# Last layer with f32 weights that hold their scales, and four context buffers, in a two-block transformer kernel on one core

## The chip, the core and the metric

The kernel runs on one NeuronCore of a Trainium2 chip. PE is the matrix engine, DVE the vector engine, ACT the scalar engine, POOL is GpSimd, and SP only issues transfers. Each engine executes its instructions in program order and waits on semaphores for what other engines or transfers deliver. Data moves by DMA: SP, ACT and POOL each have a queue, and all queues are served by the same 16 DMA engines. The metric is the time of one execution in microseconds; less is better. The profile's span runs from the first to the last instruction of one profiled execution.

## The reference, cut to what matters

There are 16 batches of 112 rows of 256 numbers, each with a context of 375 rows of 256. Four layers are added to the rows one after the other: attention with 16 heads over the context, a feed-forward layer with two routed experts and a shared one, a second attention with one head over the same context, and a quantized linear layer. Only the last two matter here:

```python
x = x + _L1_xattn_ref(_layernorm(x), ctx_1024, ctx_1024, mask)

# the quantized layer, on x2 = layernorm(x) of all rows
x_scale = jnp.maximum(jnp.abs(x2).max() / 127.0, EPS)
x_int8 = jnp.clip(jnp.round(x2 / x_scale), -128, 127)
acc_i32 = dot(x_int8, weight_int8.T)
out = acc_i32 * x_scale * weight_scale.T + bias
x = x + out
```

The scale of the last layer is one number over all rows of all batches, so no product of that layer can start before the last batch's norm is known.

## The kernel before

All schedules are written out by hand. The first attention is cut into units, four for each batch, and `unit(u)` runs one step. Work of other layers is put beside it with `at(u, f, ...)` and `mid(u, f, ...)`, which hang a call on step `u`. After the last unit the steps go on up to `LAST`: first the slots of the second half of the expert layer, then the second attention of batches 8 to 15.

**The slots.** Rows are sorted by expert into slots of 128 rows. `slot_run` runs one slot, with its expert weights `ew` (two transfers of 1 MB, started by `slot_weights`) and stores its result in `y_s` (`slot_store`). From `FIRST_RUN` on there is one slot in each step, eight in all. Between and after them lie the four quarters of the shared expert for the last chunk of rows (`ph_sh`, `hT_sh`, `acc_sh`). Once all of `y_s` is stored, POOL gathers its rows for each batch (`sort_get`, the tile `got`), and adds them to `x` (`sort_add`, line 843).

**The second attention.** `stages(k)` runs in step `STEP_0 + k`, and works on several batches at once: batch 8+k computes its scores (`second_2`, tiles `pe` and `e`), the one before it transposes its probabilities (`second_3`), the one before that multiplies them with the context (`second_4`) and starts the norm of the last layer (`norm_steps`). A stage later come that norm's rows (`xn_l`) and their largest magnitude (`third_max`). Only then are they transposed into `x3T` (`third_turn`, done four stages after the scores).

Each batch needs its context twice: `ctxT`, transposed, 128 partitions with 3000 bytes each (line 130), and `ctx`, 125 partitions with three pieces of 1024 bytes (line 121). Both are about 384 KB, and SP issues both. There are three buffers for `ctxT` and five for `ctx`. The first three batches' pairs hang on steps `STEP_0 - 7` to `STEP_0 - 5`; from stage 0 on, stage k issues the pair of batch 11+k. The same queue takes the store of the last chunk of `x` (line 804), the loads of batches 13 to 15 from it (`load_xs`, line 809) and, in stage 1, `x3T` for batches 0 to 7, 896 KB (line 1244).

**The last layer.** After the norm of batch 15 the largest magnitude is reduced over partitions by a transpose (`pm`) and spread by a matmul with ones (`pb`), which gives `xscale` and its reciprocal `rscale`. `keep_warm` issues matmuls whose results nobody reads. Then the batches go in eight pairs through three functions: `scaled` multiplies a pair of `x3T` by `rscale` and adds a constant that rounds it (on ACT or DVE); `products` takes the constant off again on ACT, which writes the pair as bf16 (`xi`), and multiplies it with the integer weights `wi_sb` in bf16; `stored` multiplies by `wsx`, the weight scales times `xscale` (DVE), adds the residual (DVE or POOL) and stores the pair.

Of the kernel before, what the change touches and what calls it, by code (L numbers as in the profile page):

```python
# [9 lines left out]
F32 = mybir.dt.float32  # L10
I32 = mybir.dt.int32
BF16 = mybir.dt.bfloat16
I8 = mybir.dt.int8
U8 = mybir.dt.uint8
AF = mybir.ActivationFunctionType
ALU = mybir.AluOpType
# [3 lines left out]
P = 128  # L20
B, S, D = 16, 112, 256
SK = 375
# [4 lines left out]
DC = D // P  # L27
# [10 lines left out]
ROUND = 1.5 * 2.0**23  # L38
# [16 lines left out]
TAIL = 8  # L55
# [3 lines left out]
def tile_kernel(  # L59
# [26 lines left out]
    nc = tc.nc  # L86
# [4 lines left out]
    ctxp = ctx.enter_context(tc.tile_pool(name="ctx", bufs=2))  # L91
# [10 lines left out]
    def gen(name):  # L102
        return ps_gen.tile([P, 512], F32, tag="gen", name=name)
# [3 lines left out]
    xall = const.tile([P, B, D], F32, tag="x", name="x")  # L107
    xt = [xall[:, t, :] for t in range(NT)]
    xs_place = [b if b < B - 4 else b ^ 2 for b in range(B)]
# [7 lines left out]
    ctx_nat, ctxT, ctxT2 = {}, {}, {}  # L117
# [8 lines left out]
        dma.dma_start(out=ctxT[b], in_=ctx_t[b])  # L126

    def load_ctxT2(b):
        ctxT2[b] = late(ctxp, 2, 3, [P, DC, SK], "ctxT_2", f"ctxT2_{b}")
        nc.sync.dma_start(out=ctxT2[b], in_=ctx_t[b])  # L130

    def weight(src, name, dma, pool=wpool):
# [71 lines left out]
    wi_sb = const.tile([P, DC, D], BF16, tag="wi", name="wi")  # L204
# [38 lines left out]
    fin = []  # L243

    def late(pool, bufs, more, shape, tag, name):

        pool, bufs = (fin[0], more) if fin else (pool, bufs)
        return pool.tile(shape, F32, tag=tag, name=name, bufs=bufs)
# [73 lines left out]
    def transposed(dst, src, name):  # L322

        pt = gen(f"pt_{name}")
        n = src.shape[0]
        for c in range(DC):
            nc.tensor.transpose(
                pt[:, c * n : (c + 1) * n], src[:, c * P : (c + 1) * P], ident[:n, :n]
            )
        nc.scalar.copy(dst, pt[:, : DC * n].rearrange("p (c s) -> p c s", c=DC))  # L330
# [571 lines left out]
    x3T = []  # L902
# [10 lines left out]
    def third_turn(bs):  # L913
        for b in bs:
            if b < TAIL:
                t = tmp.tile([P, DC, S], F32, tag="x3s", name=f"x3s_{b}", bufs=1)
                transposed(t, normed["l3", b], f"x3_{b}")
                nc.scalar.dma_start(out=x3T_d[b], in_=t)
            else:
                transposed(x3T[0][:, b, :, :], normed["l3", b], f"x3_{b}")  # L920
# [69 lines left out]
    def small_const(src, name, dtype=F32):  # L990
# [16 lines left out]
        out=wi8_sb, in_=wi8_t.rearrange("(c p) n -> p c n", p=P)  # L1007
# [4 lines left out]
    FIRST_RUN = NU + 6  # L1012
    STEP_0 = FIRST_RUN + NT // 2 + 5
# [4 lines left out]
    def at(u, f, *a):  # L1018
        extra[u].append((f, a))
# [65 lines left out]
    s = sorts[0]  # L1085
# [34 lines left out]
    s = sorts[1]  # L1120
# [41 lines left out]
    for b in range(TAIL, B):  # L1162

        at(FIRST_RUN + 3 if b < 13 else STEP_0 + b - 13, load_xs, b)
    for i in range(3):
        at(STEP_0 - 7 + i, load_ctxT2, TAIL + i)
        at(STEP_0 - 7 + i, load_ctx, TAIL + i)

    make_kT(0, 0, True)
    for i in range(GB):  # L1170
# [56 lines left out]
    def keep_warm(count):  # L1227

        pi = gen("warm")
        for _ in range(count):  # L1230
            nc.tensor.matmul(pi[:, :P], ident, ident, start=True, stop=True)

    for u in range(NU + 3):
# [1 line left out]
    first_att.close()  # L1235
    fin.append(ctx.enter_context(tc.tile_pool(name="final", bufs=1)))
    x3T.append(fin[0].tile([P, B, DC, S], F32, tag="x3T", name="x3T"))
    ws_bc = fin[0].tile([S, D], F32, tag="wscale", name="wscale")
    nc.gpsimd.dma_start(out=ws_bc, in_=wscale.partition_broadcast(S))
    rounding = fin[0].tile([P, 1], F32, tag="rounding", name="rounding")  # L1240
    nc.vector.memset(rounding, ROUND)
    at(
        STEP_0 + 1,
        lambda: nc.sync.dma_start(
            out=x3T[0][:, :TAIL, :, :].rearrange("p b c s -> p b (c s)"),
            in_=x3T_d.rearrange("b p c s -> p b (c s)"),
# [7 lines left out]
    def stages(k):  # L1254
        def b_of(back):
            b = TAIL + k - back
            return b if TAIL <= b < B else None

        def do(back, f):
            b = b_of(back)  # L1260
            if b is not None:
                f(b)

        def norm_steps(name, b):
            nb_on = nc.gpsimd if name == "l2" or b == B - 1 else nc.vector
            steps[name, b] = norm([b], name, True, nb_on)
            for f in steps[name, b][:3]:
                f()

        def now(f, at_k):  # L1270

            for b, own in zip(range(TAIL, B), at_k):
                if own == k:
                    f(b)

        def rows(name):
            return lambda b: steps[name, b][3]()

        no = None
        stats = lambda b: norm_steps("l2", b)  # L1280
        now(sort_get, (-4, -4, -3, -3))
        now(sort_add, (-3, -3, no, no, 1, 2, 3, 4))
        now(stats, (-2,))
        now(rows("l2"), (-1,))
        yield
        now(sort_add, (no, no, -2, -1))
        now(stats, (no, -2))
        if k == -1:
            now(rows("l2"), (no, -1))
            do(-1, second_1)  # L1290
        do(0, lambda b: second_2(b, lambda: do(-1, second_1)))
        do(4, lambda b: third_turn([b]))
        do(1, second_3)
        do(3, rows("l3"))
        now(rows("l2"), (no, no, 0, 1, 2, 3, 4, 5))
        do(2, second_4)
        if k == B - TAIL + 1:

            amax1.append(const.tile([S, 1], F32, tag="amax1", name="amax1"))
            do(3, lambda b: third_max([b]))  # L1300
            nc.vector.tensor_reduce(amax1[0], amax[:, : B - 1], AX.X, ALU.max)
        do(2, lambda b: norm_steps("l3", b))
        now(sort_get, (no, no, no, no, -1, 0, 1, 2))
        now(stats, (no, no, -1, 0, 1, 2, 3, 4))
        if k >= 0:
            do(-3, load_ctxT2)
            do(-3, load_ctx)
        if k != B - TAIL + 1:
            do(3, lambda b: third_max([b]))
        yield  # L1310

    for u in range(NU + 3, LAST - 1):
# [3 lines left out]
        k = u - STEP_0  # L1316
# [12 lines left out]
    d, y = far[0]  # L1329
    amax1 = amax1[0]  # L1330
    nc.vector.scalar_tensor_tensor(amax1, d, y, amax1, ALU.mult, ALU.max)
    pm = gen("pm")
    nc.tensor.transpose(pm[:1, :S], amax1, ident[:S, :S])
    top = const.tile([1, 1], F32, tag="top", name="top")
    nc.vector.tensor_reduce(top, pm[:1, :S], AX.X, ALU.max)
    keep_warm(2)
    pb = gen("pb")
    nc.tensor.matmul(pb[:, :1], ones[0:1, :], top, start=True, stop=True)
    xscale = const.tile([P, 1], F32, tag="xscale", name="xscale")
    nc.vector.tensor_scalar(xscale, pb[:, :1], 1.0 / 127.0, EPS_Q, ALU.mult, ALU.max)  # L1340
    rscale = const.tile([P, 1], F32, tag="rscale", name="rscale")
    nc.vector.reciprocal(rscale, xscale)

    for _ in stages(LAST - 1 - STEP_0):
        pass
    third_turn([B - 1])
    wsx = fin[0].tile([S, D], F32, tag="wsx", name="wsx")
    nc.gpsimd.tensor_scalar(wsx, ws_bc, xscale[:S, :], None, ALU.mult)
    pfs = {}

    def scaled(pair):
        t = x3T[0][:, 2 * pair : 2 * pair + 2, :, :]

        if pair % 2 or pair == 6:
            nc.scalar.activation(t, t, AF.Identity, bias=rounding, scale=rscale)
        else:
            nc.vector.tensor_scalar(t, t, rscale, ROUND, ALU.mult, ALU.add)

    def products(pair):
        t = x3T[0][:, 2 * pair : 2 * pair + 2, :, :]  # L1360
        xi = fin[0].tile([P, 2, DC, S], BF16, tag="xi", name=f"xi_{pair}", bufs=3)
        nc.scalar.add(xi, t, -ROUND)
        pf = gen(f"pf_{pair}")
        for j in range(2):
            for c in range(DC):
                nc.tensor.matmul(
                    pf[:S, j * D : (j + 1) * D],
                    xi[:, j, c, :],
                    wi_sb[:, c, :],
                    start=(c == 0),  # L1370
                    stop=(c == DC - 1),
                )
        pfs[pair] = pf

    def stored(pair):
        y = fin[0].tile([S, 2, D], F32, tag="y", name=f"y_{pair}", bufs=4)
        nc.vector.tensor_tensor(
            y,
            pfs[pair][:S, : 2 * D].rearrange("p (j d) -> p j d", j=2),
            wsx.unsqueeze(1).to_broadcast([S, 2, D]),  # L1380
            ALU.mult,
        )
        first = xs_place[2 * pair]
        add = nc.vector if pair in (2, 5, 7) else nc.gpsimd
        add.tensor_tensor(y, y, xall[:S, first : first + 2, :], ALU.add)
        nc.sync.dma_start(
            out=out[2 * pair : 2 * pair + 2].rearrange("b s d -> s b d"), in_=y
        )

    NP = B // 2  # L1390
    scaled(0)
    scaled(1)
    for pair in range(NP + 1):
        if pair < NP:
            products(pair)
        if pair + 2 < NP:
            scaled(pair + 2)
        if pair > 0:
            stored(pair - 1)


# [57 lines left out]
```

## Time and profile before

| quantity | us |
|---|---|
| median of three runs (967.94 to 969.63) | 969.3 |
| the profiled execution | 970.18 |
| its span | 968.4 |
| PE busy | 925.2 |
| DVE busy | 494.3 |
| ACT busy | 465.9 |
| POOL busy | 463.8 |

A view of the profile gives, for each instruction, its start, its duration, its engine, its line, what it writes and reads, and in brackets the idle time before it and what ended that idle time. The mean granted clock of PE over the span was 0.986 of full speed. It was half in two stretches after 900 us, from 917.4 to 924.3 and from 944.7 to 955.0, and again from 961.8 on.

The page's busy digits show how the last slices differ from the rest. Each digit is the busy share of one fortieth of the span, in tenths:

```profile
PE   8999999999999999999999999899999999999683
DVE  5655855464545444653444434577576442322464
ACT  4766565366535554564353442554545641221453
POOL 4766664366536544553242334666555622201743
```

PE's rows are full until the last three slices, about 73 us, in which the second attention of batches 8 to 15 and the last layer run. There no engine is busy all the time, and what matters is who waits for whom.

### The profile page before, as it was taken

How to read it: one execution, taken by the hardware profiler on the slowest of the kernel's cores; microseconds unless marked ns; L12 is line 12 of the kernel's file. 1: busy time of each engine (PE TensorE's matmuls, PEld its weight loads, DVE VectorE, ACT ScalarE, POOL GpSimd, SP SyncE). 2: the span in 40 equal slices, each digit the busy share in tenths (PEclk: the TensorE clock that was granted, in tenths of full speed). 3: DMA queues.
4: the chain of work that ended last, by engine and by line, in shares of the span. 5: the costliest groups of instructions: out<-in, count | busy, mean ns of one | idle time of the engine just before them, and what ended most of it. 6: DMA issues, size and time to landing. Idle time of an engine off the chain costs nothing. (4 is left out here: it accounts for less than half of the span.)

```text
span 968.4 us, 16839 instructions
## 1 busy us (share of the span) xinstructions
PE 925.2 (96%) x5567; PEld 706.4 (73%) x5567; DVE 494.3 (51%) x1276; ACT 465.9 (48%) x1241; POOL 463.8 (48%) x504
## 2 busy tenths in 40 slices
PE   8999999999999999999999999899999999999683
PEld 5677677777777777778778787667767678899462
DVE  5655855464545444653444434577576442322464
ACT  4766565366535554564353442554545641221453
POOL 4766664366536544553242334666555622201743
PEclk9999999999999999999999999999999999999996
DMA  5654543243326422332645522645335720586522
GB/s 185 161 164 95 136 129 74 71 101 92 74 74 197 121 70 52 77 83 59 217 159 179 205 50 70 161 127 139 95 77 133 201 59 30 201 325 220 151 96 76
DMA packets 119911, 120.69 MB, mean 125 GB/s; under 512 B 15807, under 2 KB 107153, under 8 KB 115089
## 3 DMA queue, kind: packets, MB, share of 16 engines
q1 hardware_dynamic: 107664, 97.52, 35.8%
q10 hardware_dynamic: 8144, 11.20, 4.0%
q0 software_dynamic: 4016, 10.90, 3.7%
q8 instruction: 45, 0.74, 0.3%
q14 instruction: 42, 0.34, 0.1%
HBM read 71.19 MB, written 10.62 MB: 84 GB/s over the span
## 5 line engine op out<-in xcount | busy, mean ns | idle before, releaser
L455 POOL TENSOR_SCALAR p<-p,rden 128x375 f32<-128x375 f32 x256 | 315.1, 1244 | 258.4 <-DVE rden L452 251.3
L443 ACT ACTIVATE p<-sc,nmax 128x375 f32<-128x375 f32 x256 | 143.4, 571 | 174.9 <-DVE nmax L434 169.6
L338 PE MATMUL pk<-ctxT,wk 128*128 128x375 f32 x512 | 192.1, 497 | 4.3 <-ACT kT L347 2.3
L359 PE MATMUL pv<-wv,ctxT 128*128 128x256 f32 (+1 forms) x768 | 187.0, 380 | 0.4 <-ACT kT L347 0.4
L359 PEld LDWEIGHTS pv<-wv,ctxT 128*128 128x128 f32 (+1 forms) x768 | 143.3, 187 | 47.9 <-ACT kT L347 1.6
L504 ACT COPY pT<-blk 32x384 f32<-32x384 f32 x256 | 130.0, 508 | 29.2 <-DMA pT<-blk 26.9
L476 DVE STREAM_TRANSPOSE blk<-p 128x384 f32<-128x384 f32 x256 | 132.2, 552 | 7.4 <-POOL p L455 4.5
L338 PEld LDWEIGHTS pk<-ctxT,wk 128*128 128x128 f32 x512 | 90.3, 191 | 55.7 <-issue 9.9
L434 DVE TENSOR_REDUCE nmax<-sc 128x2 f32<-128x750 f32 x128 | 111.8, 911 | 0.6 <-PE sc L426 0.5
L514 PEld LDWEIGHTS pa<-pT,v 128*64 128x64 f32 (+1 forms) x1536 | 74.4, 136 | 33.3 <-issue 15.8
L426 PE MATMUL sc<-kT,qT 64*128 64x375 f32 x512 | 98.1, 501 | 0.0
L514 PE MATMUL pa<-pT,v 128*64 128x112 f32 (+1 forms) x1536 | 88.3, 263 | 2.2 <-DMA pT<-blk 1.4
L372 DVE COPY v<-pv 119x256 f32<-119x256 f32 x64 | 27.0, 423 | 122.5 <-PE pv L359 101.3
L347 ACT COPY kT<-pk 128x375 f32<-128x375 f32 x128 | 61.3, 479 | 47.0 <-PE pk L338 47.0
L426 PEld LDWEIGHTS sc<-kT,qT 64*128 64x128 f32 x512 | 43.9, 186 | 34.1 <-issue 13.5
L770 DVE TENSOR_SCALAR hT_sl<-ph_sl,slot_b 128x128 f32<-128x128 f32 x64 | 22.3, 349 | 69.3 <-PE ph_sl L760 69.3
L760 PE MATMUL ph_sh<-ffn_x,sw 128*128 128x256 f32 x224 | 56.0, 381 | 0.0
L747 PE MATMUL acc_sh<-sw,hT_sh 128*128 128x256 f32 x224 | 55.5, 379 | 0.3 <-ACT hT_sh L772 0.3
L395 PE MATMUL pq<-xT,wq 128*128 128x224 f32 x256 | 54.2, 354 | 0.0
L772 ACT ACTIVATE hT_sl<-ph_sl,slot_b 128x128 f32<-128x128 f32 x64 | 23.2, 367 | 60.6 <-PE ph_sl L760 49.2
L443 ACT ACTIVATION_READ_ACCUMULATOR p<-sc,nmax 128x1 f32 x256 | 51.8, 202 | 0.0
L542 PE MATMUL po<-wo,oT 128*128 128x256 f32 x224 | 50.8, 380 | 0.1
(221 smaller groups left out, 1148.1 us busy)
## 6 DMA issues: line engine op xcount, KB each, us to landing
pT<-blk SPq DMA_DIRECT2D x732, 48.0 KB
ctxT<-in_ctx_t SPq DMA_DIRECT2D x31, 375.0 KB
ctx<-in_ctx SPq DMA_DIRECT2D x16, 375.0 KB
ew<-in_w ACTq DMA_DIRECT2D x2, 1024.0 KB
x_s<-idle POOLq DMA_DIRECT2D x2, 1024.0 KB, 5.8
sw<-in_sw ACTq DMA_DIRECT2D x2, 1024.0 KB
row<-x_s SPq DMA_DIRECT2D x16, 128.0 KB
y_s<-yrow SPq DMA_DIRECT2D x16, 128.0 KB
```

What stands on the lines that cost most here:

```text
L338: nc.tensor.matmul(pk[:, :SK], wk_sb[:, dc, m * P : (m + 1) * P], ctxT[b][:, dc, :], start=(dc == 0), stop=(dc == DC - 1),)
L347: nc.scalar.copy(t, pk[:, :SK])
L359: nc.tensor.matmul(pv[: KP[c], n * UD : (n + 1) * UD], ctxT[b][:, dc, c * P : c * P + KP[c]], wv_sb[:, dc, k * UD : (k + 1) * UD], start=( ...
L426: nc.tensor.matmul(sc[:, j, :SK], qT[g, m][r, i * P : (i + 1) * P], kT[b, m][r, :], start=True, stop=True,)
L434: nc.vector.tensor_reduce(nmax, sc[:, :, :SK], AX.X, ALU.max, negate=True)
L443: nc.scalar.activation(p[:, :SK], sc[:, j, :SK], AF.Exp, bias=nmax[:, j : j + 1], accum_out=den[:, j : j + 1])
L455: nc.gpsimd.tensor_scalar(p, p, rden[:, j : j + 1], None, ALU.mult)
L476: nc.vector.transpose(blocked[u][:, :, h * 32 : (h + 1) * 32], probs[u][h].rearrange("p (n k) -> p n k", k=32),)
L504: nc.scalar.copy(pT[r, :, i, :], of[r, :, i, :])
L514: nc.tensor.matmul(pa[j * DH : (j + 1) * DH, j2 * S : (j2 + 1) * S].rearrange("p (i q) -> p i q", q=QB), vv[b, k][: KP[c], c, h * DH : (h ...
L747: nc.tensor.matmul(self.acc[:n, i, :D], hT[:, i * n : (i + 1) * n], self.wb[:, f, :], start=(f == 0), stop=(f == FC - 1),)
L760: nc.tensor.matmul(ph[:, : self.n], self.wa[:, dc, f * P : (f + 1) * P], self.src[:, dc, :], start=(dc == 0), stop=(dc == DC - 1),)
```

## The change

1. *Four buffers for `ctxT`.* The first four pairs of contexts, for batches 8 to 11, now hang on steps `STEP_0 - 8` to `STEP_0 - 5`, and from stage 0 on, stage k issues the pair of batch 12+k. In SP's order each pair stands one place earlier. Batch 8's pair comes right after the store of the fifth slot and before the weights of the last slot.
2. *f32 weights.* POOL multiplies the integer weights by their scales once, in step `FIRST_RUN + 1`, into `wi_f`, an f32 tile. The scales are loaded for 128 partitions instead of 112.
3. *Scaling and rounding.* `quantized` scales a pair, adds the constant and takes it off again with two instructions of one engine, in place, in f32. Pairs go to DVE (0 and 2), ACT (1, 3, 5, 7) and POOL (4 and 6), and pair 0 goes batch by batch. There is no `xi`. All pairs are issued before the first product.
4. *Products and stores.* The products are f32. `stored` multiplies by `xscale` and adds the residual in one DVE instruction. The last pair is finished batch by batch, and the last store is issued by ACT.
5. *Order at the end.* The transposes of batch 14 (`third_turn`) move from the last stage, after `pb`, to the stage before it. There are seven warm-up matmuls ahead of `pm`, one after it, one after `pb` and four after the transposes of batch 15, where there were two between `pm` and `pb`.

```diff
-        ctxT2[b] = late(ctxp, 2, 3, [P, DC, SK], "ctxT_2", f"ctxT2_{b}")
+        ctxT2[b] = late(ctxp, 2, 4, [P, DC, SK], "ctxT_2", f"ctxT2_{b}")
...
-    for i in range(3):
-        at(STEP_0 - 7 + i, load_ctxT2, TAIL + i)
-        at(STEP_0 - 7 + i, load_ctx, TAIL + i)
+    for i in range(4):
+        at(STEP_0 - 8 + i, load_ctxT2, TAIL + i)
+        at(STEP_0 - 8 + i, load_ctx, TAIL + i)
...
+    wi_f = fin[0].tile([P, DC, D], F32, tag="wi_f", name="wi_f")
+    for c in range(DC):
+        at(FIRST_RUN + 1, nc.gpsimd.tensor_tensor, wi_f[:, c, :], wi_sb[:, c, :], ws_bc, ALU.mult)
...
-        do(4, lambda b: third_turn([b]))
+        if k < B - TAIL + 2:
+            do(4, lambda b: third_turn([b]))
...
             nc.vector.tensor_reduce(amax1[0], amax[:, : B - 1], AX.X, ALU.max)
+            do(3, lambda b: third_turn([b]))
...
-            do(-3, load_ctxT2)
-            do(-3, load_ctx)
+            do(-4, load_ctxT2)
+            do(-4, load_ctx)
...
+    keep_warm(7)
     pm = gen("pm")
     nc.tensor.transpose(pm[:1, :S], amax1, ident[:S, :S])
+    keep_warm(1)
     top = const.tile([1, 1], F32, tag="top", name="top")
     nc.vector.tensor_reduce(top, pm[:1, :S], AX.X, ALU.max)
-    keep_warm(2)
     pb = gen("pb")
     nc.tensor.matmul(pb[:, :1], ones[0:1, :], top, start=True, stop=True)
+    keep_warm(1)
...
+    keep_warm(4)
+
+    def quantized(on, t):
+
+        if on is nc.scalar:
+            nc.scalar.activation(t, t, AF.Identity, bias=rounding[:, 0:1], scale=rscale)
+            nc.scalar.activation(t, t, AF.Identity, bias=rounding[:, 1:2])
         else:
-            nc.vector.tensor_scalar(t, t, rscale, ROUND, ALU.mult, ALU.add)
+            on.tensor_scalar(t, t, rscale, ROUND, ALU.mult, ALU.add)
+            on.tensor_scalar(t, t, -ROUND, None, ALU.add)
+
+    def products(b, pf, j):
+        for c in range(DC):
+            nc.tensor.matmul(
+                pf[:S, j * D : (j + 1) * D],
+                x3T[0][:, b, c, :],
+                wi_f[:, c, :],
+                start=(c == 0),
+                stop=(c == DC - 1),
+            )
+
+    def stored(pf, b, n, queue=nc.sync):
+        j = b % 2
+        y = fin[0].tile([S, 2, D], F32, tag="y", name=f"y_{b}", bufs=5)[:, :n]
+        first = xs_place[b]
+        nc.vector.scalar_tensor_tensor(
+            y,
+            pf[:S, j * D : (j + n) * D].rearrange("p (j d) -> p j d", j=n),
+            xscale[:S, :],
+            xall[:S, first : first + n, :],
+            ALU.mult,
+            ALU.add,
+        )
+        queue.dma_start(out=out[b : b + n].rearrange("b s d -> s b d"), in_=y)
+
+    by = [nc.vector, nc.scalar, nc.vector, nc.scalar, nc.gpsimd, nc.scalar, nc.gpsimd, nc.scalar]
...
+    for b in range(2):
+        quantized(by[0], x3T[0][:, b, :, :])
+    for pair in range(1, B // 2):
+        quantized(by[pair], pair_of(pair))
+    for pair in range(B // 2):
+        pf = gen(f"pf_{pair}")
+        for j in range(2):
+            products(2 * pair + j, pf, j)
+        if pair < B // 2 - 1:
+            stored(pf, 2 * pair, 2)
+        else:
+            stored(pf, 2 * pair, 1)
+            stored(pf, 2 * pair + 1, 1, nc.scalar)
```

More of the change, by code (lines that the diff above doesn't have):

```diff
@@ L1237, in tile_kernel @@
     x3T.append(fin[0].tile([P, B, DC, S], F32, tag="x3T", name="x3T"))
[L1238 to L1241, printed above, removed]
+    ws_bc = fin[0].tile([P, D], F32, tag="wscale", name="wscale")
+    nc.gpsimd.dma_start(out=ws_bc, in_=wscale.partition_broadcast(P))
+    wi_f = fin[0].tile([P, DC, D], F32, tag="wi_f", name="wi_f")
+    for c in range(DC):
+        at(FIRST_RUN + 1, nc.gpsimd.tensor_tensor, wi_f[:, c, :], wi_sb[:, c, :], ws_bc, ALU.mult)
+    rounding = fin[0].tile([P, 2], F32, tag="rounding", name="rounding")
+    nc.vector.memset(rounding[:, 0:1], ROUND)
+    nc.vector.memset(rounding[:, 1:2], -ROUND)
     at(
@@ L1346, in tile_kernel @@
     third_turn([B - 1])
[L1347 to L1355, printed above, removed]
-        else:
-            nc.vector.tensor_scalar(t, t, rscale, ROUND, ALU.mult, ALU.add)
[L1359 to L1362, printed above, removed]
+    keep_warm(4)
@@ L1363, in products @@
+    by = [nc.vector, nc.scalar, nc.vector, nc.scalar, nc.gpsimd, nc.scalar, nc.gpsimd, nc.scalar]
+    pair_of = lambda pair: x3T[0][:, 2 * pair : 2 * pair + 2, :, :]
+    for b in range(2):
[3 more added lines that the diff above has]
+    for pair in range(B // 2):
         pf = gen(f"pf_{pair}")
         for j in range(2):
[L1365 to L1399, printed above, removed]
+            products(2 * pair + j, pf, j)
[4 more added lines that the diff above has]
+            stored(pf, 2 * pair + 1, 1, nc.scalar)
 def kernel(**inputs):
```

## The prediction

> **What bounds the kernel now.** I read the busy table first: PE is busy 96% of the span, but the edits lie in the last tenth of it, where that average says little. So I went to the chain of waits from 886 us on, then to the timeline of that stretch, the queue of SP, the table by stretch, and the landing events that the trace keeps for each transfer (one per DMA engine used). First the chain, in order of time (start, us, what):
>
> ```profile
> 889.87 0.04 POOLq L829
> ...
> 890.75 0.86 POOL got L829
> ...
> 907.11 12.69 DMA ctxT<-in_ctx_t
> 919.80 0.14 issue
> 919.94 2.81 PE pe L857 x4
> ...
> 953.12 2.65 POOL y L1385 x2
> ```
>
> Three things set the end. The gathers `got` start at 889.87, as soon as the last store of `y_s` has landed (889.80). PE waits for `ctxT` of batch 12 until 919.94. And in the last layer engines hand pairs to each other. How SP queues the transfers:
>
> ```profile
> 865.92 0.33 SPq L823 DMA_DIRECT2D y_s<-yrow  x1
> 871.40 0.34 SPq L709 DMA_DIRECT2D ew_(7, 4)_8475<-in_w  x1
> 872.70 0.33 SPq L709 DMA_DIRECT2D ew_(7, 4)_8477<-in_w  x1
> 873.22 0.33 SPq L823 DMA_DIRECT2D y_s<-yrow  x1
> 873.60 0.43 SPq L130 DMA_DIRECT2D ctxT<-in_ctx_t  x1
> 874.08 0.37 SPq L121 DMA_DIRECT2D ctx<-in_ctx  x1
> ```
>
> The table by stretch (last two columns: DMA share, GB/s) shows what a context load does:
>
> ```profile
> 873.10:880.50 7.40, 7.40 (x54) 6.99 (x53) 2.11 (x7) 1.72 (x6) 0.00 (x0) 1.00 0.90 341
> 885.50:887.50 2.00, 2.00 (x12) 1.77 (x11) 0.83 (x2) 0.00 (x0) 0.00 (x0) 1.00 0.34 119
> 617.30:620.50 3.20, 0.92 (x7) 0.54 (x5) 2.93 (x9) 2.69 (x10) 1.75 (x3) 1.00 0.98 257
> 620.50:623.90 3.40, 3.35 (x6) 2.08 (x7) 0.97 (x3) 1.46 (x5) 3.40 (x4) 0.50 0.83 218
> ```
>
> At 885.5 to 887.5 only `ctx` rows move: 34% of 16 engines, about five, at 119 GB/s. The landing events agree: a `ctx` load ends on five engines. And each engine keeps the queue's order: the `y_s` store issued at 880.47 landed on eleven engines by 882.17, on the other five at 883.89 to 885.45, each 0.26 after the `ctx` ahead of it.
>
> **Part 1, the early context pair.** Four buffers let batch 8's `ctxT` and `ctx` be issued one step earlier: behind the `y_s` store of 865.92, ahead of both last expert weights. Every later pair moves up one place, so three pairs instead of two stand before the last `y_s` store (887.49). Per pair on those five engines: `ctx` 384 KB / 119 = 3.2 us, `ctxT` 24 KB at 24 GB/s = 1.0; together 4.2. Before, they were busy without a gap from about 873 to 889.45; at 871.7 to 873.1 the share was 0.65, so only some 0.2 of the 4.2 fills a gap on the latest engine. The last `y_s` store lands **4.0 later** (3.2 if 1.0 us of gap is filled; 4.4 if `ctx` goes as slowly as on the latest engine). The gathers wait for all of it, and so on through bn, root, `xn_l` at 898.31, the `hT_sh` queued behind it on ACT, `acc_sh` at 899.32, `pe` at 901.95: no slack. The last expert weights landed at 880.20 for a first use at 881.09; some 3 us later, PE waits about 2 (0 to 3), which lies under the 4.0.
>
> **Part 2, the removed stall.** Batch 12's `ctxT` now goes in the place of batch 11's (issued 905.26, landed 909.8), ahead of the 896 KB of `x3T`. `pe` of 12 starts when PE is free, at 914.27: 5.7 us gone. What is late next is a row that the edit doesn't move:
>
> ```profile
> 919.94 2.81 PE L857 MATMUL pe<-ctxT,xT 128*112 128x375 f32 x4 [5.67 <-DMA ctxT<-in_ctx_t]
> 923.70 0.73 POOL L843 TENSOR_TENSOR x<-x,got 112x256 f32<-112x256 f32 x1 [4.20 <-DMA x<-x_d]
> ```
>
> The rows of batch 15 (SP at 911.48) land at 923.56 with the same transfers ahead of them as before (one `ctxT`, `ctx`, `x3T`, another pair). POOL adds them until 924.43; DVE, in order, then runs `bn_l` at 924.45 instead of 926.67, and `nmax` of batch 13, queued behind, at 925.5 instead of 927.50. ACT's `exp` and norm rows follow by the same amount. So **2.0** of the 5.7 remains (0.3 to 5.7). The next `ctxT` loads take places that landed at 919.80, 924.71 and 929.08, for uses at about 919.9, 924.1 and 931: at most 0.7 of PE, which is not late there.
>
> **Part 3, the last layer.** Products become f32. Rows:
>
> ```profile
> 899.32 1.99 PE L747 MATMUL acc_sh<-sw,hT_sh 128*128 128x256 f32 x8 [0.29 <-ACT hT_sh L772]
> 956.54 1.11 PE L1366 MATMUL pf<-wi,xi 128*112 128x256 bf16 x8 [0.47 <-ACT xi L1362]
> ```
>
> An f32 product is two records of 0.217 ((1.99 - 0.25) / 8), so 32 products take 13.9 us at full clock; in bf16 they took 0.139 each, 4.4, hidden behind scaling and evictions. A rule that speaks against the change is in the Trainium skill, "FP8 and Floating Point Precision", TensorE Precision Notes: true f32 goes through the array four times. Four times 0.139 would be 17.8, worse by 3.9; the row says 3.1 times, and I take the row. Start: batch 14's transposes leave the queue behind `pb` (947.38) for a place two products earlier, and warm-up matmuls fill the gap in which the clock fell (half from 944.7 to 955.0). At full clock `pb` ends some 0.9 sooner, `rscale` at 946.97, the first half pair is rounded by 947.5; PE ends its warm-up and batch 15's transposes at 948.1. Products end at 962.0, the last step in DVE (0.48, as L897's 112x256) at 962.5; before, the last add ended at 962.52. The last store is half as large: -0.3. Supply is early: ACT eight ops of 0.75 by 953.7, POOL four of 1.66 (0.95 for 256 columns) by 953.7, needed at 958.5 and 960.3; DVE's step, 0.7 per pair, fits in PE's 1.74. So **-0.3** (-0.8 if PE starts at 947.5; +3.4 if two clock windows are half). With one answer: `wi_f`, two POOL ops of about 0.8, lies in POOL's 56.28 of idling before the gathers; the wider `wscale` load and a memset lie beside the slots' matmuls.
>
> **Part 4, the clock.** PE gets new gaps: before `hT_sh` about 2.7 us (4.0 - 2 + 0.69), with 0.9 of work inside, and about 2.4 between `pe` of 14 (done 926.3) and batch 15's turn (928.6). The Trainium skill, "TensorE: Matmul & The Clock Gate", Part 1, lets the clock fall after a whole idle window of about 3.4 us: neither gap is one, cost 0. But the rows at 617.3 and 620.5 above show it halved for 3.4 us after a stretch with 0.92 of 3.20 busy. By that row each gap has about an even chance, at up to 1.7 (half of 3.4). I take one, **+1.0** on the path (0 to 3.4).
>
> **Sum** against the profiled execution: +4.0 - 2.0 - 0.3 + 1.0 = **+2.7**: span 968.4 to 971.1, with the 1.8 outside it 972.9 for 970.18. That execution stood 0.9 above the median, so the median 969.3 becomes **972.0**.
>
> **Rivals.**
> - *Cancelled*: the queue costs its lower 3.2, no clock window falls: +0.9, 970.2. For it: both gaps are shorter than a window. Chance 0.22.
> - *The queue delay is absorbed* (the faster side): eleven engines have the store through 1.5 us after its issue; if the five also found gaps in the 20 us between, so that the delay is under 0.4, only -2.3 is left: 967.0. Against it: the gathers started 0.07 after the last engine's landing, and the five showed no gap. Chance 0.13.
> - *The whole stall goes*: batch 15's rows don't bind, -5.7 in place of -2.0: 4.0 - 5.7 - 0.3 = -2.0, 967.3. Against it: POOL idled 4.20 for them. Chance 0.07.
> - *The f32 products run at half clock* for two windows on top: +3.4, 975.4. Against it: warm-up matmuls cover 943.5 to 948.1. Chance 0.13.
>
> The forecast keeps 0.45, with 970.6 to 974 as its own range. A measurement here tells about 0.2%, 1.9 us, from no change. Faster: the second and third, 0.20; same: the first, 0.22; slower: 0.58. The range 967.3 to 975.2 reaches into both outer cases and leaves out under 0.2.
>
> **What would show it.** In the changed profile: SP issues a context pair before the last expert load, PE waits 1 to 3 us for that load, and the first gather starts about 4 us later against the stores' issue; `pe` of batch 12 no longer waits for `ctxT`, but POOL still waits for `x<-x_d`; the f32 products stand back to back at 0.87 per batch from warm-up to end. I am wrong if the gathers start on time, if POOL's wait for the rows is gone, or if the products take much else than 13.9 us.

## The result and the profile after

| | before | after |
|---|---|---|
| median of 18 runs each (us) | 969.23 | 972.55 |
| lowest and highest | 965.0, 972.4 | 968.69, 978.13 |
| profiled execution, its span | 970.18, 968.4 | 975.31, 973.6 |

The ratio is 1.0043 with a 95% interval of 1.003 to 1.0056: slower, by 3.3 us between the medians. The profiled execution of after stands 2.8 above the median of its kernel, so its own sum is not the median's.

First the chain of waits of after from 872 us on (start, us, what; dots stand for links left out):

```profile
872.52 11.95 DMA ew_(7, 4)_8483<-in_w
884.51 2.93 PE ph_sl L760 x12
...
895.09 1.74 DMA y_s<-yrow
...
897.74 4.91 DMA got<-y_s,batch_place
...
907.01 1.99 PE acc_sh L747 x8
...
909.63 1.53 PE pe L857 x4
...
919.25 11.66 DMA x<-x_d
...
937.49 2.56 PE pa L888 x6
940.05 2.02 PE pe L857 x4
...
955.68 14.04 PE pf L1369 x64
```

Two of before's three links have changed. `ctxT` of batch 12 is gone, and the rows of batch 15 (`x<-x_d`) stand in its place. POOL's adds of the last layer are gone, and the f32 products stand there. New at the head are the last slot's weights. The timeline of SP shows why these are late:

```profile
867.09 0.33 SPq L823 DMA_DIRECT2D y_s<-yrow  x1
867.46 0.43 SPq L130 DMA_DIRECT2D ctxT<-in_ctx_t  x1
867.93 0.40 SPq L121 DMA_DIRECT2D ctx<-in_ctx  x1
872.52 0.36 SPq L709 DMA_DIRECT2D ew_(7, 4)_8483<-in_w  x1
873.82 0.34 SPq L709 DMA_DIRECT2D ew_(7, 4)_8485<-in_w  x1
```

The pair now stands ahead of both weights. The rows that wait, in the timeline of after (the bracket is the idle time before and what ended it), and then its products in the table of groups (busy us, mean ns):

```profile
884.51 2.93 PE L760 MATMUL ph_sl<-slot_x,ew_(7, 4)_8483 128*128 128x128 f32 x12 [3.34 <-DMA ew_(7, 4)_8483<-in_w]
...
931.04 0.72 POOL L843 TENSOR_TENSOR x<-x,got 112x256 f32<-112x256 f32 x1 [3.91 <-DMA x<-x_d]
...
933.25 1.56 PE L857 MATMUL pe<-ctxT,xT 128*112 128x375 f32 x4 [2.83 <-DVE nmax L871]
```

```profile
L1369 PE MATMUL pf<-wi_f,x3T 128*112 128x256 f32 x64 | 14.0, 380 | 0.0
```

PE waits 3.34 for the weights. POOL still waits 3.91 for the rows of batch 15, and PE, through DVE's `nmax`, 2.83. The products run without a gap. The table by stretch of after (length; then PE, PEld, which is PE's weight loads, DVE, ACT and POOL busy, each with its number of instructions; granted clock; DMA share; GB/s) shows what the waits cost in clock:

```profile
880.00:883.00 3.00, 1.17 (x6) 0.69 (x4) 0.74 (x2) 0.00 (x0) 0.00 (x0) 1.00 0.97 354
883.00:886.00 3.00, 1.49 (x7) 1.49 (x8) 0.00 (x0) 0.18 (x1) 0.00 (x0) 0.57 0.49 196
886.00:888.00 2.00, 2.00 (x9) 1.91 (x9) 0.35 (x1) 0.56 (x2) 0.00 (x0) 0.50 0.89 266
888.00:891.00 3.00, 3.00 (x15) 2.68 (x14) 0.35 (x1) 0.29 (x1) 0.00 (x0) 0.63 0.40 122
891.00:894.00 3.00, 3.00 (x22) 2.79 (x21) 0.70 (x2) 0.45 (x2) 0.00 (x0) 1.00 0.34 116
```

In the first wait the clock falls to half, and it stays there from 883.4 to 890.2. A second fall, from 934.6 to 941.4, follows the wait before `pe` of batch 14; in the same view:

```profile
931.00:934.60 3.60, 1.35 (x4) 0.63 (x4) 2.60 (x9) 1.06 (x4) 3.20 (x7) 1.00 0.34 109
934.60:938.00 3.40, 2.36 (x10) 2.03 (x10) 1.93 (x7) 2.82 (x8) 1.51 (x4) 0.50 0.32 109
938.00:941.40 3.40, 3.40 (x8) 2.19 (x8) 1.46 (x7) 0.72 (x2) 0.06 (x1) 0.50 0.04 14
```

All profiles can be cut at the same three places: the issue of the first weights of the slot before the last (`ew_(7, 3)`), the first score matmul of batch 8 (`pe`), the transpose `pm` that begins the last layer's scale, and the end of the span. For before the cuts are 864.10, 901.95, 945.71 and 968.4. The lengths A, B and C between them leave out what earlier parts of an execution add. All experiments stand in the same table. The ratio is that to the kernel before on the same chip. "Gathers" is the first `got` after the first cut, and the clock is the mean over the span of the profiled execution.

| kernel | ratio (95% interval) | gathers | A | B | C | clock |
|---|---|---|---|---|---|---|
| before | 1 | 26.65 | 37.85 | 43.76 | 22.69 | 0.986 |
| after | 1.0043 (1.003–1.0056) | 32.47 | 44.36 | 43.55 | 20.42 | 0.990 |
| e1 last layer alone | 0.9982 (0.9965–0.9999) | 26.21 | 37.92 | 42.34 | 20.43 | 0.996 |
| e2 contexts alone | 1.0056 (1.0037–1.0075) | 32.04 | 43.24 | 40.94 | 22.73 | 0.985 |
| e3 pairs one place later | 0.9998 (0.998–1.0016) | 27.22 | 40.18 | 40.47 | 20.40 | 0.998 |
| e4 a late POOL op | 1.0082 (1.005–1.0114) | 31.95 | 43.13 | 40.65 | 23.74 | 0.993 |
| e5 rows of 14, 15 first | 1.0017 (0.9997–1.0036) | 31.47 | 42.67 | 40.56 | 20.42 | 0.997 |
| e6 before, POOL ends early | 0.9986 (0.9972–1.0) | 26.06 | 37.49 | 42.51 | 19.86 | 0.992 |
| e7 warm-up under the wait | 1.0023 (1.001–1.0036) | 32.14 | 43.32 | 41.91 | 20.35 | 0.998 |
| e8 last layer, late x3T | 0.9957 (0.9941–0.9974) | 26.01 | 37.55 | 40.78 | 20.44 | 1.000 |
| e9 only ctxT earlier | 0.9993 (0.9975–1.001) | 28.87 | 40.05 | 41.41 | 20.47 | 0.998 |
| e10 as e8, four buffers | 0.9966 (0.9949–0.9983) | 27.99 | 39.17 | 41.14 | 20.47 | 0.997 |
| e11 before, POOL early, late x3T | 0.9941 (0.9919–0.9963) | 26.36 | 37.63 | 39.46 | 20.59 | 0.991 |
| e12 ctx on all engines | 0.9953 (0.9931–0.9974) | 27.87 | 39.26 | 38.46 | 20.42 | 1.000 |

Behind the first cut the profile of after is 4.0 longer than that of before: 6.5 in A, -0.2 in B and -2.3 in C. The other 1.2 between the two spans lie ahead of the cut.

### The profile page after: what moved, and what is told of

It reads as the page before. It is cut to its first block, busy times and chain, and to the rows that moved or that the text cites. A ratio compares the mean times of both kernels' runs of the same rounds, so it can differ in the third digit from the quotient of the medians.

```text
span 973.6 us, 16946 instructions
## 1 busy us (share of the span) xinstructions
PE 938.8 (96%) x5621; PEld 717.0 (74%) x5621; DVE 493.9 (51%) x1278; ACT 463.8 (48%) x1236; POOL 461.1 (47%) x504
## 5 line engine op out<-in xcount | busy, mean ns | idle before, releaser
L514 PEld LDWEIGHTS pa<-pT,v 128*64 128x64 f32 (+1 forms) x1536 | 74.3, 136 | 32.5 <-issue 15.5
```

The costliest lines, as they stand in the source:

```text
L514: nc.tensor.matmul(pa[j * DH : (j + 1) * DH, j2 * S : (j2 + 1) * S].rearrange("p (i q) -> p i q", q=QB), vv[b, k][: KP[c], c, h * DH : (h ...
```

## Experiments: the two halves apart

**e1**, after with the contexts of before:

```diff
-        ctxT2[b] = late(ctxp, 2, 4, [P, DC, SK], "ctxT_2", f"ctxT2_{b}")
+        ctxT2[b] = late(ctxp, 2, 3, [P, DC, SK], "ctxT_2", f"ctxT2_{b}")
...
-    for i in range(4):
-        at(STEP_0 - 8 + i, load_ctxT2, TAIL + i)
-        at(STEP_0 - 8 + i, load_ctx, TAIL + i)
+    for i in range(3):
+        at(STEP_0 - 7 + i, load_ctxT2, TAIL + i)
+        at(STEP_0 - 7 + i, load_ctx, TAIL + i)
...
-            do(-4, load_ctxT2)
-            do(-4, load_ctx)
+            do(-3, load_ctxT2)
+            do(-3, load_ctx)
```

> The last layer's edit alone; the context pairs stand as they stood before. Theory (from the two traces): everything up to amax as before, and the tail from amax to the end of the span 2.2 us shorter (20.6 against 22.8), mostly because POOL's closing DRAIN, which ran from 960.7 to 967.65 and ended last, now starts 2.8 us earlier and lies under the stores: 967.0 against 969.2. The prediction's own term: -0.3, so 968.9. Rival: f32 products cost more than they save: 970 or above.

966.72 against 967.91. A is that of before, and C is 2.3 shorter: the last layer's edit by itself gains 1.2 by the medians and about 1.7 by the ratio (0.0018 of 969).

**e2**, before with the opposite of these lines, and nothing else:

> The four context buffers alone, on the kernel before. Theory: PE waits 3 us for the last slot's weights behind the early pair, the half clock after that wait costs another 3, batch 12's wait gives 2 to 2.5 back, the tail's gain is missing: +4 to +6, 973.2 to 975.2. In its trace: pe of batch 8 some 5 to 7 us later than before, POOL's DRAIN last at the end. The prediction's own terms: +4.0 - 2.0 + 1.0 = +3.0, 972.2. Rival (the edit pays and the last layer loses): 967 to 969.

973.3, or +5.4 by the ratio. A is 5.4 longer than before's, C is before's. B is 2.8 shorter than before's, 1.4 shorter than that of e1, which has before's three buffers. The two halves add up: -1.7 + 5.4 = +3.7, and after has +4.2 by its ratio.

## Experiments: what the early pair costs

**e7**, after with matmuls that nobody reads ahead of the last slot, so that PE doesn't stand idle while the weights are under way:

```diff
+        if j == s.slots - 1:
+            at(u, lambda: keep_warm(12))
         at(u, slot_run, s, i)
```

> After, with 12 warm-up matmuls (24 records of 0.13, 3.1 us) on PE ahead of the last slot, where it waits 2.2 to 3.3 for the slot's weights. Theory (half of the early pair's cost is the clock that falls behind that wait: slot 4 took 9.9 to 10.1 from its first matmul to its end, 7.7 without a wait): slot 4 back at 7.7 to 8.0, the last y_s store and all behind it 2 earlier: +2 on before instead of +4. Rival (the clock has another cause, or the warm-up delays the slot by as much): within 0.5 of after.

The clock stayed at 1.00 in that stretch. The slot took 9.05 from its first matmul to the issue of its store, against 10.58 in after. The time is what the theory gave (+2.2 by the ratio), but it did not come the theory's way: the gathers came at 32.14, only 0.3 earlier than in after. The rows of the timeline and the table by stretch of e7 show what holds the gathers (the releasers in the brackets are inferred; the landing events below say more):

```profile
879.85 1.60 PE L760 MATMUL ph_sl<-slot_x,ew_(7, 4)_8483 128*128 128x128 f32 x12
...
893.56 0.99 POOL L829 DMA_INDIRECT got<-y_s,batch_place  x1 [61.47 <-DVE hT_sh L770]
```

```profile
885.00:888.00 3.00, 3.00 (x21) 2.77 (x20) 0.70 (x2) 0.37 (x1) 0.00 (x0) 1.00 0.34 120
```

PE is busy all of the time and the queue has a third of its engines at work. The last store, issued at 888.90, has landing events on eleven engines from 890.44 to 890.60 and on the other five from 891.16 to 892.65. So it is the queue of five engines that holds the gathers here, and PE's wait lies under it. It is the same in e2, e4 and e5, where the last of the sixteen engines landed 2.8 to 3.5 after the issue.

The profile of after itself is a tie. Its slot was so slow that the store, issued at 895.09, landed on all sixteen engines by 896.83; the five had ended the `ctx` rows ahead of it at 896.49. A faster slot would have gained little: whether the slot took 9.0 (e5, e7), 9.5 (e2, e4) or 10.6 (after), the gathers came 31.5 to 32.5 behind the first cut.

The run was nevertheless 1.9 faster than after by the ratios, though their intervals overlap. Its mean clock, 0.998 in the median of its runs against 0.994 for after, is a likely reason and not a shown one: no profile shows the runs that make up these medians.

**e12**, after with each `ctx` of batches 8 to 15 in two transfers, in the same place of the queue:

```diff
-        nc.sync.dma_start(out=t, in_=ctx_in[b].rearrange("(c p) d -> p c d", p=KC))
+        rows = ctx_in[b].rearrange("(c p) d -> p c d", p=KC)
+        for part in [slice(0, KC)] if b < TAIL else [slice(0, 112), slice(112, KC)]:
+            nc.sync.dma_start(out=t[part], in_=rows[part])
```

> After, with each ctx load of batches 8 to 15 in two parts, 112 rows and 13 rows, in the same places of SP's queue. Theory (the early pair delays the last y_s store because the 125 rows of a ctx load go to five DMA engines only, with eleven idle): 112 rows spread over 16 engines and 13 over 13, so that a ctx costs about 1.0 of each engine's queue as ctxT does; the store lands 2.7 after its issue, the gathers come within 1.5 us of before's place (after ew_3: 26.0 to 27.6, where after has 32.5), PE waits less than 1 for the last slot's weights. With the gain behind it (-2.3) and the tail (-1.7): -2.5 to -4 on before, ratio 0.996 to 0.9975. Rival (it is the bytes ahead of the last weights, on any number of engines): gathers at 30 or later, ratio 1.002 or above.

962.99 against 968.27, faster than expected. The table by stretch of e12, PE's one wait for the weights, and the row of the first gather:

```profile
879.00:882.00 3.00, 2.24 (x14) 2.14 (x15) 0.35 (x1) 0.15 (x1) 0.00 (x0) 1.00 1.10 275
882.00:885.00 3.00, 3.00 (x21) 2.80 (x20) 0.70 (x2) 0.58 (x2) 0.00 (x0) 1.00 0.47 100
885.00:888.00 3.00, 3.00 (x16) 2.64 (x15) 0.96 (x2) 0.47 (x1) 0.00 (x0) 1.00 0.26 64
```

```profile
879.76 0.67 PE L749 MATMUL acc_sl<-ew_(7, 4)_8486,hT_sl 128*128 128x256 f32 x2 [1.45 <-DMA ew_(7, 4)_8486<-in_w]
```

```profile
888.73 0.99 POOL L831 DMA_INDIRECT got<-y_s,batch_place  x1 [57.19 <-DMA ctx<-in_ctx]
```

The long tail on five engines is gone. The `ctx` ahead of the last store had landed by 885.51, and the store, issued at 886.23, landed on all sixteen engines between 887.77 and 887.94. The gathers came at 27.87, 4.6 earlier than in after, if a little later than the 26.0 to 27.6 expected. PE waited nothing for the slot's first weights and 1.45 for its second, where less than 1 was expected. The Trainium skill, "DMA: Bandwidth & Descriptors", "Why a DMA increments its semaphore by 16 and not by 1", says that a transfer uses the largest number of engines up to 16 that divides the slowest dimension of both its sides: by this rule 125 rows give five, and 112 give sixteen. The landing events agree with both. Most of the early pair's cost is therefore its 125 rows. Its bytes still cost PE the 1.45; the 1.2 by which the gathers stay behind before's lie within the spread of the kernels with before's order (26.0 to 28.0), so this remainder isn't settled.

The rest of the gain lies in B, at 38.46 the shortest of all, for the edit also splits the later loads. In after the rows of batch 15, issued at 919.25, were on eleven engines by 924.59 but on the other five only at 929.25 to 930.91, each behind a `ctx`; in e12, issued at 910.26, they had landed by 916.88, and nobody waited for them. So the same five engines were behind the wait of POOL. The kernel before with its contexts split was not run: how much of e12's time the split would give there is open.

**e9**, after with `ctxT` one step earlier and `ctx` where it was:

```diff
-        at(STEP_0 - 8 + i, load_ctx, TAIL + i)
+    for i in range(3):
+        at(STEP_0 - 7 + i, load_ctx, TAIL + i)
...
-            do(-4, load_ctx)
+            do(-3, load_ctx)
```

> After, but only ctxT goes one step earlier; each ctx is issued where it was before the change. Theory (the early pair's cost is its ctx rows, which only five engines take; ctxT is spread over all and costs 1.0 of queue): the gathers come 1 us later than in before instead of 5.4, the wait of pe 12 for ctxT is gone, the rows of 15 still bind, the tail's gain stays: +1 - 2.3 - 1.7 = -3 on before, ratio 0.996 to 0.998 where after has 1.0043. Rival (any load ahead of the last weights costs as much, ctxT too): A store 3 or more late, ratio 1.001 or above.

966.84, 1.5 below before by the medians and 0.7 by the ratio: less than the 3 expected. The gathers came at 28.87, 2.2 later than in before's profile, where 1 was expected. That term isn't sharp: e10, with before's order of transfers, has its gathers at 27.99, and in both the five engines held the last store, for up to 4.0 and 3.7 after its issue.

**e3**, after with the first four pairs one step later, so that batch 8's pair follows the last weights again and batch 11's pair follows the last store:

```diff
-        at(STEP_0 - 8 + i, load_ctxT2, TAIL + i)
-        at(STEP_0 - 8 + i, load_ctx, TAIL + i)
+        at(STEP_0 - 7 + i, load_ctxT2, TAIL + i)
+        at(STEP_0 - 7 + i, load_ctx, TAIL + i)
```

> After, but batch 8's pair goes behind the last expert weights again, as before, and batch 11's pair follows the last y_s store at once (four buffers still). Theory: the cost of the early pair goes and the gain at batch 12 stays: pe of 8 at before's time, no wait of pe 12 for ctxT, POOL's wait for the rows of batch 15 stays; -2.0 to -2.5 there and -2.2 in the tail: 964.0 to 965.5. Rival 1: the gain at batch 12 is worth nothing by itself, 967. Rival 2: the cost was not the pair's place: 970 to 973, like after.

967.7: the first rival's number, for another reason. B is as short as expected (40.47). But A is 2.3 longer than before's. Batch 11's pair, issued right behind the last store, moves together with the gathers, which is the likely reason. In the timeline of e3 POOL waits for what was gathered:

```profile
897.30 1.40 POOL L843 TENSOR_TENSOR x<-x,got 112x256 f32<-112x256 f32 x2 [1.82 <-DMA got<-y_s,batch_place]
```

The first gather started at 890.77, so 6.53 passed until this add; in before 4.74 passed.

## Experiments: what is late behind the removed wait

**e5**, after with the rows of batches 13 to 15 all loaded in stage 0:

```diff
-        at(FIRST_RUN + 3 if b < 13 else STEP_0 + b - 13, load_xs, b)
+        at(FIRST_RUN + 3 if b < 13 else STEP_0, load_xs, b)
```

> After, with the rows of batches 14 and 15 loaded together with those of 13, ahead of batch 12's context pair and of x3T. Theory (the prediction's own: once the wait for ctxT is gone, the rows of batch 15 bind): POOL's wait of 3.2 to 3.9 for x<-x_d goes, with it PE's 2.2 to 2.8 before pe of 14; -2 to -3 on after, so +1.3 to +2.3 on before. Rival: the rows only end a wait that something else would end at once: -0.5 to 0 on after, +3.5 to +4.2 on before.

970.08, in the expected range. But the profile doesn't bear out the way there. POOL's wait for the rows is gone, and B is 40.56, as it was in e4 with that wait (40.65): now PE waits 1.88, 0.76 and 0.37 for `ctxT` of later batches. What the profile does lack are the two falls of the clock. Rows and contexts share one queue, and whichever stands behind is late.

**e8**, the kernel of e1 with `x3T`, which only the last layer reads, loaded four steps later:

```diff
     at(
-        STEP_0 + 1,
+        STEP_0 + 5,
         lambda: nc.sync.dma_start(
```

> The last layer's edit with three context buffers (as in the first of these runs), and x3T, 896 KB that only the last layer reads, loaded four steps later, behind all context pairs. Theory (both waits, for ctxT of batch 12 and for the rows of 15, come from x3T's place in SP's queue): both go without any early pair; -1.7 as the first run, and a further -2.5 to -3: 963.5 to 964.5 for 969.2, ratio 0.994 to 0.996. Rival (three buffers hold batch 12's pair back in any case): no further gain, ratio 0.998.

963.9 against 968.41. Nobody waits for the rows, PE waits 1.46 and 1.39 for `ctxT`, and B is 40.78 with three buffers, as short as with four. What the fourth buffer was to bring, a different order brings without the early pair. **e10**, the same with four buffers and nothing moved:

> The last layer's edit and the late x3T, with a fourth ctxT buffer and nothing moved: SP need not wait for a buffer before it issues a ctxT load. Theory: what is left of waits for ctxT with three buffers (1.46 and 1.39 on PE in that profile) goes; -0.5 to -1.5 on the same kernel with three, ratio 0.994 to 0.995. Rival (those waits lie beside DVE's and ACT's chain and are worth nothing): ratio 0.9955 to 0.9965, as with three.

965.33, not below e8. Its profile still has a wait of 1.93 for `ctxT`. A fourth buffer by itself is worth nothing that these runs can tell.

## Experiments: the tail

**e4**, after with one copy of eight columns on POOL, which waits for the `y` of the last store but one:

```diff
         queue.dma_start(out=out[b : b + n].rearrange("b s d -> s b d"), in_=y)
+        if b == B - 2:
+            last = fin[0].tile([S, 8], F32, tag="last", name="last")
+            nc.gpsimd.tensor_copy(last, y[:, 0, :8])
```

> After, with one tiny copy on POOL that waits for the last pair's y (some 970.6 in the span). Nothing is left out and nothing waits for the copy. Theory: POOL's closing DRAIN ends about 7 us after the start of POOL's last operation and the kernel waits for it: 977.6 + 0.5 against 973.6, so +4 to +4.5 on after, 976.5 to 977. Rival: the DRAIN's 7 us belong to something else (a fixed cost hidden beside the stores, or the length of the operation before it): 0 to +0.3, 972.5 to 972.9.

976.98, +7.9 by the ratio where after has +4.2: 3.7, with a wide interval from six runs, for a copy that takes 0.19 and that nothing waits for. In the profiles C is 3.3 longer. **e6**, before with pair 6's residual add on DVE:

```diff
-        add = nc.vector if pair in (2, 5, 7) else nc.gpsimd
+        add = nc.vector if pair in (2, 5, 6, 7) else nc.gpsimd
```

> Before, with the residual add of pair 6 on DVE in place of POOL, so that POOL's last operation is pair 4's add. Theory (POOL's closing DRAIN sets before's end, some 6 us after the end of POOL's last operation): the DRAIN falls under the stores, the end follows the last store: -2.4, with +0.5 for the add that DVE takes on: -1.9. Rival (the end is the stores' in any case): 0 to +0.5.

966.72 against 968.41, -1.4 by the ratio, with an interval that reaches 1. In the profiles C is 2.8 shorter. POOL's last operation in before and in e4:

```profile
960.71 1.26 POOL L1385 TENSOR_TENSOR y<-y,x 112x512 f32<-112x512 f32 x1 [1.23 <-DVE y L1377]
```

```profile
964.08 0.19 POOL L1392 COPY last<-y 112x8 f32<-112x8 f32 x1 [11.00 <-DVE y L1381]
```

The closing instructions of before, after, e4 and e6, in this order (durations in ns as least/median/most, then the first and the last start in us) show what ends when:

```profile
L1455 POOLq DRAIN  x3: 46/104/6948, 960.7 to 968.2; - x3
L1455 SPq DRAIN  x3: 7/7/7, 965.2 to 967.9; - x3
```

```profile
L1462 POOLq DRAIN  x3: 46/104/7038, 957.9 to 973.3; - x3
L1462 SPq DRAIN  x3: 7/7/7, 972.8 to 973.1; - x3
```

```profile
L1465 POOLq DRAIN  x3: 46/104/5862, 964.1 to 970.5; - x3
L1465 SPq DRAIN  x3: 7/7/7, 966.5 to 970.2; - x3
```

```profile
L1455 POOLq DRAIN  x3: 46/104/7417, 953.9 to 962.2; - x3
L1455 SPq DRAIN  x3: 7/7/7, 961.6 to 961.9; - x3
```

SP's first DRAIN starts when the last store has landed (in before 965.2 for 965.02, in after 972.8 for 972.61). POOL's first DRAIN lasts 5.9 to 7.4 us. In before it ran from 960.7 to 967.65, 2.4 beyond SP's 965.2, and everything else waited. In after it ended at 964.95, far below 972.8. In e4 it ended at 969.96, 3.5 beyond SP. In e6 it ended at 961.3, just below SP's 961.6.

**e11**, e6 with the late `x3T`, so with bf16 products:

> Before, with bf16 products, three buffers, the residual add of pair 6 on DVE (so that POOL ends early) and x3T four steps later. Theory: the last layer's edit gains through POOL's earlier end alone, and the f32 products give nothing by themselves (tail 19.9 here in the profile with that add on DVE, 20.4 with f32 products): as fast as the f32 last layer with the late x3T, ratio 0.995 to 0.997. Rival (the f32 products in one step are worth a microsecond or more): ratio 0.998 or above.

962.87 against 968.31, the lowest ratio of all and a little below the range expected, with an interval that overlaps e8's and e12's. It lies apart from the interval of e6, from which this kernel differs only in the place of `x3T`. C is 20.59 here and 19.86 in e6, against 20.42 with f32 products. Beside e8, which has the f32 layer and the same order of loads, it shows no gain of the f32 layer beyond POOL's early end.

## Why the prediction was right, by its steps

The forecast was +2.7 and the medians stand 3.3 apart. The direction and its causes were right: the early pair costs more than the removed wait gives back. That the sum came so near is partly luck. The gain of the last layer was forecast some 2 too small, and the costs of the early pair and of the clock too small by about as much.

- **Part 1, +4.0.** The first gather came 5.4 later in e2 than in before (32.04 against 26.65). In e2, e4, e5 and e7 the five engines held the last store and PE's wait (2.67 in e2, 2.22 in e4) lay under it, as forecast; in the profile of after, with a wait of 3.34, both ended together. e12 shows that the rows of `ctx` are most of the cause. The term that was too small is the pair's 4.2. The share of `ctxT` in it was put at 1.0; e9 has it between 0.9 (against e10's 27.99) and 2.2 (against before). Why the pair costs more than 4.2 isn't settled. A reading was a little off as well: eleven engines had the earlier store 1.7 after its issue (882.17 for 880.47), not 1.5; no term of the sum rests on it.
- **Part 2, -2.0.** B fell by 2.8 in e2 against before's profile and by 1.4 against e1's. In these two `ctxT` of batch 12 was awaited 5.67 and 3.96, and the clock stood at half for 6.9 and 3.4 us around it. What was named as late next, the rows of 15, is what POOL waits for in after, e2, e3 and e4. The reason given, the transfers ahead of them in the queue, was only part of it: it is the five engines of a `ctx` that bring them late. e5 adds that with the rows moved the contexts are late again. e12 removes both waits (B 38.46); e8 removes that for the rows and keeps 1.46 and 1.39 for `ctxT` (40.78).
- **Part 3, -0.3.** C fell by 2.3, and e1 gained 1.7. Products took 14.04 (forecast 13.9; four times the bf16 product gave 17.8, so the row was the better guide), with a start 2.63 behind the end of `amax` (forecast 2.45). The missing term is the end of POOL: the sum compared the last add with the last step in DVE, as if the stores ended both kernels. Before was ended by POOL's DRAIN, 2.4 later, as e6 and e4 show by taking it away and by putting it back.
- **Part 4, +1.0.** The forecast gave each new gap an even chance of a fall of the clock, and took one. In the profiles of after, e2 and e4 the clock fell in both. None of the idle gaps of PE before these falls was longer than after's 3.34, and in after PE was busy 1.17 of 3.00 before the first fall and 1.35 of 3.60 before the second. So the row held there too against the rule of a whole idle window. Both falls lasted 6.8 us in after and 3.4 to 3.5 in e2 and e4. A is 44.36 in after, 43.24 and 43.13 in e2 and e4, and 42.67 and 43.32 in e5 and e7, which have no fall there; B is 43.55, then 40.94 and 40.65, and 40.47 in e3, which has none. So a fall of 3.4 cost little and one of 6.8 cost 1 to 3, if the waits, which differ a little, are left aside.

By these profiles the first three terms sum to +5.4 - 2.1 (the middle of 2.8 and 1.4) - 2.3 = +1.0. Of the 3.3 between the medians 2.3 are left. They are most likely the clock's, but no run isolates them. Over the 18 runs of after the time rises by 0.77 for each 0.001 that the mean clock is lower (correlation -0.79; in e1 the slope is 1.36, in e7 0.57). The median clock of after is 0.994, that of e1 0.996, that of e7 0.998; by that slope it costs after an estimated 1.5 to 3 more than these. The two runs of after with 0.998 took 968.69 and 969.07, no more than before's median. The mean clock ranks runs of one kernel and not kernels: before has 0.988 in the runs beside e1, and yet is faster than after.

Of the rivals, *absorbed* falls with e2, *the whole stall goes* with POOL's 3.91, *half clock in the products* with their 14.04 at full clock, and *cancelled* with the 5.4 of the gathers.

## What to carry to other kernels

- A load has a place in a queue and a shape that decides how many engines serve it. Before moving one earlier, ask what stands behind it on the engines it uses: 125 rows held five engines while eleven were idle, and a split into 112 and 13 rows of these and all later loads turned the same change from +4.2 to -4.6 by the ratios.
- When a transfer is late, look for one ahead of it that nobody needs yet. Moving `x3T` four steps back brought what a buffer and an early load were to bring.
- Look at the closing instructions before shortening a tail: the engine that finishes its work last need not be the one that ends the kernel.

## What the runs showed of the hardware

POOL's closing DRAIN ended 5.7 us after the end of POOL's last operation in all four kernels above (before 967.65 for an add that ended at 961.97; after 964.95 for 959.29; e4 969.96 for 964.27; e6 961.3 for 955.66), be that an add over 512 columns or a copy of eight. In these kernels POOL's last operation has to end that much ahead of the last store's landing to cost nothing.

A profile of one execution carries a few microseconds of its own: the same order of transfers (before, e1, e6, e8, e10, e11) gave gathers from 26.0 to 28.0 behind the same cut. The half-clock stretches inside the spans lasted 3.4 to 3.5 us (e1, e2, e4, e10), 6.8 to 6.9 (before, after, e6) or 10.2 to 10.3 (before, e2, e11): close to one, two or three times the same length.
